# Masking B and the scores by one product, signed sums of dt*A, and another order of the first loads in a modulated Mamba-and-experts layer

## The chip, the cores and the metric

The kernel runs on one core of a Trainium2 chip. The metric is the device time of one execution in microseconds (us); the time before is the median of three runs.

## The reference, cut to what matters

Eight sequences (`B = 8`) of 2048 tokens with 256 features, all in float32. A conditioning vector gives six modulation vectors per sequence. Then, for each sequence:

```python
h = _layernorm(x) * (1 + ca) + sa
x = x + ga * _L0_attn_ref(h, ...)        # the Mamba part
h = _layernorm(x) * (1 + cb) + sb
x = x + gb * _L0_ffn_ref(h, ...)         # 8 experts, weighted by a softmax with a threshold
```

The Mamba part projects `h` to z, xBC and dt, runs a causal convolution of four taps over xBC, applies SiLU, and does a chunked state-space scan with 8 heads of 64 channels and a state of 128:

```python
dt = softplus(dt + dt_bias);  A = -exp(A_log)
dA_cs = jnp.cumsum(dt * A, axis=2)
Lmat = where(causal, exp(dA_cs_i - dA_cs_j), 0)
scores = einsum('bcihn,bcjhn->bcijh', Cc, Bc) * Lmat
states = einsum('bcjhn,bcjh,bcjhp->bchpn', Bc, exp(dA_cs[-1] - dA_cs), xt)
y_off  = einsum('bcihn,bcih,bchpn->bcihp', Cc, exp(dA_cs), prev_states)
```

## The kernel before

The tokens are worked in 32 blocks of 512 (four per sequence), numbered 0 to 31 here; a block has four chunks of 128 tokens. Each stage of a block is a Python generator. `STARTS` gives the planned time of a stage within its block, `PERIOD` (70) the distance of blocks, and `at` and `after` put a generator into a queue of events; a `yield t` hands over to other stages for a planned `t`. Matmul results go to eight PSUM banks, which `take` hands out and `give` returns in planned time. The planned times decide only the order in which instructions are recorded and which bank each uses; the tile framework then reorders them on each engine by its own priorities, and on the chip each engine runs its list in order, held by semaphores. An engine that waits therefore holds everything behind it in its list.

The stages that the change and the prediction touch, with the lines of the profile:

- `condition` (L250) and `modulation` (L257): the conditioning vector is turned (L252), copied (L253, DVE) to `ct`, multiplied with the first modulation weights `wpp` (L262) and copied to `mod_pp` (L267, DVE).
- `first_norm` (L351): statistics of x (L315, L316, DVE), then `modulated` (L318): `rstd` by two POOL instructions (L310, and the power at L311), `shift` (L324, DVE), the normalised `xn` (L328, ACT), transposes (L338, PE), `ht` (L340, ACT). `gate_weights` (L679) calls `modulated` once more in each block, so there are two `shift` steps per block.
- `project_xbc` (L409, PE) and `conv` (L364 and L368 on ACT, three taps at L372 on DVE), `silu_xbc` (L427, ACT), `project_z` (L445, PE; SiLU at L432, ACT).
- `steps_of_time` (L454 on): dt, then `cs` = running sum of dt * `a_pos` (L486, L487), `whole` = minus its last column (L489), `e` = exp(cs + whole) (L493, ACT), three transposes (L497) and `tok_major` by three DVE copies, the second with the sign turned (L502).
- `spread` (L508): a DMA broadcasts `cs` from DRAM to all partitions as `wide` (L512).
- `within` (L517), once per chunk: `w` = Relu(wide + bias) in eight ACT instructions (L527), transposes of x (L537) and of B (L538), scores (L540), two exponentials (L541, L542), then on DVE `xdt` (L545), the masked scores `sm` (L549) and the copy `bm` of the transposed B (L551). `sm` and `bm` read the two halves of the bank `b_ps`, so that bank comes free when both are done. POOL makes `xdec` (L558) and `cw` (L565); DVE `w = w * sm` (L562); PE the new state (L576), POOL and DVE its decay and sum (L579, L590).
- `outputs` (L596): y (L608, PE), plus D times x (L620, DVE), times SiLU(z) (L624, DVE), squares (L631, ACT) and their sums on POOL (L633, L634).
- `output` (L662), `residual` (L671), `gate_weights`, and `experts` (L781 on PE; weighted sums L738 on DVE; L746, L748 on POOL).
- Loads are issued from SP's queue: the modulation weights, block 0's x as one DMA, the input weights, small vectors, and from planned times on the expert weights (`expert_weights`, L170) and the x of later blocks (`fetch`, L105).

Of the kernel before, what the change touches and what calls it, by code (L numbers as in the profile page):

```python
# [11 lines left out]
AF = mybir.ActivationFunctionType  # L12
ALU = mybir.AluOpType
AX = mybir.AxisListType

P = 128
# [9 lines left out]
def kernel(  # L26
# [26 lines left out]
    nc = tc.nc  # L53
    B, L, DM = x.shape
    NPROJ = w_in.shape[1]
    DI = w_out.shape[0]
    NH = dt_bias.shape[0]
# [7 lines left out]
    NC = T // P  # L65
    NSB = L // T
# [6 lines left out]
    def new(pool, shape, tag, bufs=None):  # L73
        n_names[0] += 1
        kw = {} if bufs is None else {"bufs": bufs}
        return pool.tile(shape, F32, tag=tag, name=f"{tag}_{n_names[0]}", **kw)
# [6 lines left out]

    ident = new(const, [P, P], "ident")
    make_identity(nc, ident)
    upper = new(const, [P, P], "upper")
    make_upper_triangular(nc, upper, val=1.0, diag=True)
    ones = new(const, [P, P], "ones")
    nc.gpsimd.memset(ones, 1.0)
    neg_half = new(const, [P, NC], "neg_half")  # L90
    nc.gpsimd.memset(neg_half, -0.5)

# [4 lines left out]
    chk = ctx.enter_context(tc.tile_pool(name="chunk", bufs=2))  # L97
    sml = ctx.enter_context(tc.tile_pool(name="small", bufs=2))
    dram = ctx.enter_context(tc.tile_pool(name="dram", bufs=2, space=bass.MemoryType.DRAM))

    def load(b, s):
        xt = new(io, [P, NC, DM], "xt")
        nc.sync.dma_start(out=xt, in_=x[b, ts(s, T), :].rearrange("(c p) d -> p c d", p=P))  # L105
        return xt

    def columns(dst, src, first, count):
        nc.sync.dma_start(
            out=dst, in_=src[:, first : first + count].rearrange("(k p) n -> p k n", p=P)  # L110
        )
# [22 lines left out]
    heads["gate_b"] = new(const, [P, NE], "gate_b")  # L134
    w_dt = new(const, [P, KD, QD], "w_dt")
    nc.gpsimd.memset(w_dt, 0.0)
    a_pos = new(const, [P, 1], "a_pos")

    columns(wpp[0], wmod, 0, 2 * DM)
    first_x = load(0, 0)  # L140
    columns(w_in_sb[:, :, DI:], w_in, DI, NPROJ - DI)
    with nc.allow_non_contiguous_dma(reason="small vectors, an element or a few per partition"):
        nc.sync.dma_start(out=conv_w_sb, in_=conv_w.rearrange("(m p) k -> p m k", p=P))
        nc.sync.dma_start(out=conv_b_sb, in_=conv_b.rearrange("(m p) -> p m", p=P))
        columns(w_in_sb[:, :, :DI], w_in, 0, DI)
        for name, v in (("dt_bias", dt_bias), ("a_log", a_log)):
            for c in range(NC):
                nc.sync.dma_start(
                    out=heads[name][c * QD : c * QD + NH, :], in_=v.unsqueeze(1)
                )  # L150
        for q in range(2):
            nc.sync.dma_start(
                out=d_ch[ts(q, HEADDIM), :],
                in_=d_skip.rearrange("(m q) -> q m", q=2)[q].partition_broadcast(HEADDIM),
            )
        nc.sync.dma_start(out=norm_sb, in_=norm_w.rearrange("(m p) -> p m", p=P))
        nc.sync.dma_start(out=wo_n, in_=w_out.rearrange("(m p) o -> p m o", p=P))
        for g, part in enumerate((2, 5)):
            columns(wgate[:, :, g, :], wmod, part * DM, DM)
        columns(wpp[1], wmod, 3 * DM, 2 * DM)  # L160
        nc.sync.dma_start(
            out=gate_w_sb[:, :, :NE], in_=gate_w.rearrange("(k p) e -> p k e", p=P)
        )
# [11 lines left out]
    def head_weights():  # L175

        nc.gpsimd.tensor_copy(w_dt[:, :, :NH], w_in_sb[:, :, DI + CD : NPROJ])
        nc.scalar.activation(a_pos, heads["a_log"], AF.Exp)
        yield


# [4 lines left out]
    def at(time, stage):  # L186
        heapq.heappush(events, (time, n_events[0], stage))
        n_events[0] += 1
# [31 lines left out]
    def give(ps):  # L220
        free_at[bank_of.pop(ps.tensor.name)] = clock[0] + READ_TIME

# [2 lines left out]
        while any(step not in d for step in steps):  # L225
            yield 0.2

    order = [(b, s) for b in range(B) for s in range(NSB)]
    info = [{} for _ in order]
    gated, carry = {}, {}  # L230

# [7 lines left out]
        return t.unsqueeze(2).to_broadcast([P, NC, NE])  # L239

    def fetch(n):
        info[n]["x"] = first_x if n == 0 else load(*order[n])
        yield


# [3 lines left out]
    def condition():  # L249
        for k in range(KD):  # L250
            ps = yield from take("m")
            nc.tensor.transpose(ps[:, :B], cond_sb[:, ts(k, P)], ident[:B, :B])  # L252
            nc.vector.tensor_copy(ct[:, k, :], ps[:, :B])  # L253
            give(ps)
        yield from modulation(0)

    def modulation(half):  # L257
        ps = yield from take("m")
        for n in range(2):
            for d in range(KD):  # L260
                for k in range(KD):
                    nc.tensor.matmul(  # L262
                        ps[:, ts(n * KD + d, B)], wpp[half][:, k, n * DM + d * P :][:, :P],
                        ct[:, k, :], start=(k == 0), stop=(k == KD - 1),
                    )
        for n in range(2):
            nc.vector.tensor_scalar(  # L267
                mod_pp[:, 2 * half + n], ps[:, ts(n, KD * B)].rearrange("p (d b) -> p d b", b=B),
                float(n), None, ALU.add,
            )  # L270
        give(ps)
# [180 lines left out]
    def steps_of_time(n):  # L452

        d = info[n]  # L454
        ht = d["ht", 0]
        dt_ps = yield from take("m")
        for k in range(KD):
            for c in range(NC):
                nc.tensor.matmul(
                    dt_ps[ts(c, QD), :P], w_dt[:, k, :], ht[:, k, ts(c, P)],  # L460
                    start=(k == 0), stop=(k == KD - 1), skip_group_check=True,
                )
        yield 1.0


        dtv = new(sml, [P, P], "dtv", bufs=1)
        e = new(sml, [P, P], "sp_e", bufs=1)
        u = new(sml, [P, P], "sp_u", bufs=1)
        ln = new(sml, [P, P], "sp_l", bufs=1)
        dt = new(sml, [P, P], "dt", bufs=1)  # L470
        nc.vector.tensor_scalar(dtv, dt_ps[:, :P], heads["dt_bias"], None, ALU.add)
        give(dt_ps)
        nc.vector.scalar_tensor_tensor(e, dtv, -1.0, dtv, ALU.mult, ALU.min)
        yield 0.6
        nc.scalar.activation(e, e, AF.Exp)
        yield 0.5
        nc.vector.tensor_scalar(u, e, 1.0, None, ALU.add)
        yield 0.3
        nc.scalar.activation(ln, u, AF.Ln)
        yield 1.8  # L480
        nc.vector.scalar_tensor_tensor(u, u, 1.0, e, ALU.subtract, ALU.subtract)
        nc.vector.scalar_tensor_tensor(dt, dtv, 0.0, ln, ALU.max, ALU.add)
        nc.vector.tensor_sub(dt, dt, u)

        cs = new(sml, [P, P], "cs", bufs=1)
        nc.vector.tensor_scalar(u, dt, a_pos, None, ALU.mult)  # L486
        nc.vector.tensor_tensor_scan(cs, ones, u, 0.0, ALU.mult, ALU.add)  # L487
        whole = new(sml, [P, 1], "whole")
        nc.vector.tensor_scalar(whole, cs[:, P - 1 : P], -1.0, None, ALU.mult)  # L489
        yield 4.0  # L490
        d["cs_d"] = new(dram, [P, P], "cs_d")
        nc.sync.dma_start(out=d["cs_d"], in_=cs)
        nc.scalar.activation(e, cs, AF.Exp, bias=whole)  # L493
        yield 7.0
        t_ps = yield from take("m")
        for i, t in enumerate((dt, cs, e)):
            nc.tensor.transpose(t_ps[:, ts(i, P)], t, ident)  # L497
        yield 1.0
        tok_major = d["tok"] = new(sml, [P, 3, NC, NH], "tok_major", bufs=3)
        turned = t_ps[:, : 3 * P].rearrange("p (n c q) -> p n c q", n=3, q=QD)  # L500
        for i, sign in enumerate((1.0, -1.0, 1.0)):
            nc.vector.tensor_scalar(  # L502
                tok_major[:, i], turned[:, i, :, :NH], sign, None, ALU.mult
            )
        give(t_ps)


# [9 lines left out]
    def within(n, c):  # L517
# [7 lines left out]
        w = new(chk, [P, NH, P], "w", bufs=3)  # L525
        for h in range(NH):
            nc.scalar.activation(  # L527
                w[:, h, :], wide[:, h, :], AF.Relu, bias=tok_major[:, 1, c, h : h + 1]
            )
            if h % 4 == 3:  # L530
                yield 1.6
# [6 lines left out]
        nc.tensor.transpose(b_ps[:, :P], bt, ident)  # L538

        nc.tensor.matmul(b_ps[:, P : 2 * P], bt, ct_, start=True, stop=True)  # L540
        nc.scalar.activation(wide, wide, AF.Exp, scale=-1.0)  # L541
        nc.scalar.activation(w, w, AF.Exp, scale=-1.0)  # L542
        yield 1.2
        xdt = new(chk, [P, DI], "xdt", bufs=3)
        nc.vector.tensor_tensor(  # L545
            by_head(xdt), by_head(x_ps[:, :DI]), per_head(tok_major[:, 0, c, :]), ALU.mult
        )
        sm = new(chk, [P, P], "sm")
        nc.vector.tensor_mul(sm, b_ps[:, P : 2 * P], upper)  # L549
        bm = new(chk, [P, P], "bm")  # L550
        nc.vector.tensor_copy(bm, b_ps[:, :P])  # L551
        give(x_ps)
        give(b_ps)
        last = s_of(n) == NSB - 1 and c == NC - 1
# [233 lines left out]


    READ_TIME = 4.5  # L790
    PERIOD, XBC_STEP, Z_STEP, OUT_STEP = 70.0, 6.0, 3.5, 4.4
    STARTS = (
        (fetch, -20.0), (first_norm, -9.0), (project_xbc, 11.5), (project_z, 42.0),
        (silu_xbc, 47.5), (output, 128.0), (gate_weights, 156.0), (experts, 198.0),
    )
    at(-30.0, condition())
    at(12.0, head_weights())
    at(35.0, expert_weights())
    at(20.0, output_weights())
    at(30.0, modulation(1))  # L800
    for n in range(len(order)):
# [42 lines left out]
```

## Time and profile before

| what | value |
|---|---|
| runs shown, median (lowest to highest) | 2406.21 us (2404.78 to 2408.36) |
| the profiled execution's own time | 2408.26 us |
| its span, first to last instruction | 2406.5 us |
| mean granted TensorE clock | 0.988 |
| PE, DVE, ACT, POOL busy | 97%, 76%, 67%, 47% |
| DMA | 110.51 MB, mean 46 GB/s |

A busy share is an average over stages. A line of the timeline gives the start, the duration, the engine, the line of the kernel, the operation with its tiles and shapes, the number of merged instructions, and in brackets the idle time before it with what ended that. "L549" is line 549 of the kernel before; the changed kernel's lines are numbered some ten higher, and this document uses the old numbers for both except in lines copied from the later profile.

### The profile page before, as it was taken

To read this page: it belongs to the slowest core of one execution; us is meant where nothing else is said; L and a number is where in the kernel's file an instruction comes from. 1 tells how busy PE (TensorE), PEld (TensorE's weight loads), DVE (VectorE), ACT (ScalarE), POOL (GpSimd) and SP (SyncE) were. 2 spreads that over 40 slices of the span, in tenths; PEclk is the share of its full clock that TensorE was granted. 3 is DMA by queue.
4 is the path that set the end of the run, shared out by engine and by line. 5 is a ranking of instruction groups with operands and counts; after the bars stand their busy time and mean duration, and the time that the engine had idled before them with its cause. 6 is when DMAs were issued, how large, how long until landed. Compare 5 with 4: busy or idle time off the path is not lost.

```text
span 2406.5 us, 33568 instructions
## 1 busy us (share of the span) xinstructions
PE 2327.3 (97%) x11602; PEld 1313.9 (55%) x11602; DVE 1830.3 (76%) x4414; ACT 1621.4 (67%) x2947; POOL 1128.7 (47%) x1244
## 2 busy tenths in 40 slices
PE   6889999999999999999999999999999999999998
PEld 3545555555555555555555555555555555555564
DVE  4777877777777787777887778777777787778775
ACT  6877676676666766667867667767677667667720
POOL 2554454443554435545445545445545445545442
PEclk8999999999999999999999999999999999999999
DMA  5111011110111101111111111111111111111100
GB/s 164 45 37 39 34 55 45 44 46 28 54 46 44 45 28 54 46 45 54 37 37 54 46 46 53 37 37 55 54 36 54 37 37 54 46 44 45 37 18 18
DMA packets 64601, 110.51 MB, mean 46 GB/s; under 512 B 7048, under 2 KB 47024, under 8 KB 64432
## 3 DMA queue, kind: packets, MB, share of 16 engines
q1 hardware_dynamic: 64416, 108.35, 13.3%
q8 instruction: 93, 1.52, 0.3%
q14 instruction: 76, 0.62, 0.1%
q10 hardware_dynamic: 16, 0.01, 0.0%
HBM read 89.47 MB, written 18.87 MB: 45 GB/s over the span
## 4 chain that ended last, share of the span: by engine, by line
PE 61%; ACT 11%; DVE 7%; POOL 6%; issue 1%; POOLq 0%; ACTq 0%
PE bank L781 26%; PE bank L662 8%; PE bank L409 7%; PE bank L445 6%; PE bank L608 4%; PE bank L576 3%; ACT w L527 3%; DVE xbc L372 2%; POOL cw L565 2%; PE bank L338 1%; PE bank L537 1%; ACT xn L328 1%; POOL rstd L311 1%; ACT wide L541 1%; DVE res L738 1%
## 5 line engine op out<-in xcount | busy, mean ns | idle before, releaser
L781 PE MATMUL bank<-we_sb,ht 128*128 128x512 f32 x2048 | 968.7, 598 | 18.3 <-DVE bm L551 15.6
L738 DVE SCALAR_TENSOR_TENSOR res<-bank,wt,res 128x256 f32<-128x256 f32 x1024 | 487.3, 476 | 212.6 <-PE bank L781 116.5
L781 PEld LDWEIGHTS bank<-we_sb,ht 128*128 128x128 f32 x2048 | 375.5, 191 | 398.8 <-issue 351.8
L372 DVE SCALAR_TENSOR_TENSOR xbc<-bank,conv_w_sb,xbc 128x511 f32<-128x511 f32 (+2 forms) x576 | 425.4, 740 | 96.0 <-ACT halo L368 94.9
L565 POOL TENSOR_TENSOR cw<-wide,xbc 128x1024 f32<-128x1024 f32 x128 | 305.7, 2388 | 274.5 <-ACT wide L541 157.2
L527 ACT ACTIVATE w<-wide,tok_major 128x128 f32<-128x128 f32 x1024 | 327.2, 390 | 137.8 <-PE bank L608 96.2
L409 PE MATMUL bank<-ht,w_in_sb 128*128 128x512 f32 x768 | 375.1, 611 | 5.6 <-DVE xbc L372 4.5
L445 PE MATMUL bank<-ht,w_in_sb 128*128 128x512 f32 x512 | 244.6, 601 | 1.0 <-ACT zs L432 1.0
L662 PE MATMUL bank<-wo,zs 128*128 128x256 f32 x1024 | 244.0, 380 | 0.3
L579 POOL TENSOR_TENSOR state<-state,wide 128x512 f32<-128x512 f32 x112 | 120.8, 1079 | 247.1 <-DVE state L590 216.7
L409 PEld LDWEIGHTS bank<-ht,w_in_sb 128*128 128x128 f32 x768 | 141.9, 194 | 163.6 <-issue 142.1
L340 ACT ACTIVATE ht<-bank,mod_pp 128x512 f32<-128x512 f32 x128 | 97.7, 776 | 188.9 <-PE bank L338 188.8
L364 ACT ACTIVATE xbc<-bank,conv_b_sb,conv_w_sb 128x512 f32<-128x512 f32 x192 | 147.3, 767 | 113.9 <-PE bank L409 113.0
L662 PEld LDWEIGHTS bank<-wo,zs 128*128 128x128 f32 x1024 | 189.9, 191 | 51.2 <-issue 26.4
L746 POOL TENSOR_TENSOR res<-res,gates 128x256 f32<-128x256 f32 x128 | 133.4, 1042 | 149.2 <-DVE res L738 142.4
L558 POOL TENSOR_TENSOR xdec<-xdt,tok_major 128x512 f32<-128x512 f32 x120 | 139.0, 1159 | 132.7 <-DVE xdt L545 130.5
L328 ACT ACTIVATE xn<-xt,shift,rstd 128x256 f32<-128x256 f32 x256 | 137.1, 591 | 89.2 <-DVE shift L324 89.2
L620 DVE SCALAR_TENSOR_TENSOR bank<-xbc,d_ch,bank 128x128 f32<-128x128 f32 x512 | 176.6, 349 | 20.7 <-PE bank L608 11.8
L562 DVE TENSOR_TENSOR w<-w,sm 128x1024 f32<-128x1024 f32 x128 | 189.0, 1477 | 0.0
L633 POOL TENSOR_TENSOR sq<-sq 128x256 f32<-128x256 f32 x128 | 99.2, 775 | 124.4 <-ACT sq L631 124.2
L445 PEld LDWEIGHTS bank<-ht,w_in_sb 128*128 128x128 f32 x512 | 91.0, 191 | 97.6 <-issue 90.6
L576 PE MATMUL bank<-xdec,bm 128*128 128x512 f32 x240 | 130.1, 625 | 12.7 <-POOL xdec L558 6.4
(129 smaller groups left out, 3364.6 us busy)
## 6 DMA issues: line engine op xcount, KB each, us to landing
wide<-cs_d SPq DMA_DIRECT2D x128, 512.0 KB
xt<-_attn_hidden_states_dram SPq DMA_DIRECT2D x32, 512.0 KB
out_dram<-xt SPq DMA_DIRECT2D x32, 512.0 KB
we_sb<-in_L_ffn_expert_w_dram SPq DMA_DIRECT2D x8, 256.0 KB
cs_d<-cs SPq DMA_DIRECT2D x32, 64.0 KB
ht<-in_L_wmod_dram SPq DMA_DIRECT2D x2, 512.0 KB
w_in_sb<-in_L_attn_W_in_dram SPq DMA_DIRECT2D x1, 776.0 KB
w_in_sb<-in_L_attn_W_in_dram SPq DMA_DIRECT2D x1, 512.0 KB
```

The lines of the kernel that those rows point to most:

```text
L328: nc.scalar.activation(xn[:, c, :], src[:, c, :], AF.Identity, bias=shift[:, c : c + 1], scale=rstd[:, c : c + 1],)
L372: nc.vector.scalar_tensor_tensor(acc[:, ahead:], ps[:, : T - ahead], conv_w_sb[:, m, k : k + 1], acc[:, ahead:], ALU.mult, ALU.add,)
L409: nc.tensor.matmul(ps, w_in_sb[:, k, DI + m * P : DI + (m + 1) * P], ht[:, k, :], start=(k == 0), stop=(k == KD - 1),)
L445: nc.tensor.matmul(ps, w_in_sb[:, k, ts(m, P)], ht[:, k, :], start=(k == 0), stop=(k == KD - 1),)
L527: nc.scalar.activation(w[:, h, :], wide[:, h, :], AF.Relu, bias=tok_major[:, 1, c, h : h + 1])
L562: nc.vector.tensor_tensor(w, w, sm[:, None, :].to_broadcast([P, NH, P]), ALU.mult)
L565: nc.gpsimd.tensor_tensor(cw, wide, ct_[:, None, :].to_broadcast([P, NH, P]), ALU.mult)
L576: nc.tensor.matmul(st_ps[:, :DI], bm, xdec, start=True, stop=True)
L620: nc.vector.scalar_tensor_tensor(y[:, m, :], xbc[:, m, tok], d_ch[:, m : m + 1], y[:, m, :], ALU.mult, ALU.add,)
L662: nc.tensor.matmul(o_ps[:, :DM], d["zs"][:, m, ts(c, P)], wo[:, m, :], start=(m == 0), stop=(m == MI - 1),)
L738: nc.vector.scalar_tensor_tensor(res, ps[:, ts(q, DM)], wt[:, c, e + q : e + q + 1], res, ALU.mult, ALU.add)
L781: nc.tensor.matmul(ps, ht[:, k, ts(c, P)], we_sb[:, k, e : e + per, :].rearrange("p e o -> p (e o)"), start=(k == 0), stop=(k == KD - 1),)
```

## The change

The `upper` mask and the `ones` become two halves of one tile, so that one DVE product over 256 columns makes B (times ones) and the masked scores (times upper) where there were a product and a copy of 128 columns each. dt * A is summed with its negative sign, so that the turned sums need no change of sign: three copies to `tok_major` become one, `whole` goes, and the signs move into scales of ACT instructions; one small POOL instruction negates exp(A_log) once. At the start, block 0's x is loaded first, as four DMAs, block 1's x is loaded among the weights, and the expert weights' planned time goes from 35 to 60. `ct` is copied by ACT instead of DVE. The first modulation's copies are recorded later, and 15 products of the two masks that nobody reads (`warm`) are put on PE.

```diff
-    upper = new(const, [P, P], "upper")
+    masks = new(const, [P, 2, P], "masks")
+    ones, upper = masks[:, 0, :], masks[:, 1, :]
...
+    first_x = new(io, [P, NC, DM], "xt")
+    for c in range(NC):
+        nc.sync.dma_start(out=first_x[:, c, :], in_=x[0, ts(c, P), :])
     columns(wpp[0], wmod, 0, 2 * DM)
-    first_x = load(0, 0)
     columns(w_in_sb[:, :, DI:], w_in, DI, NPROJ - DI)
...
+        second_x = load(*order[1])
         nc.sync.dma_start(out=norm_sb, in_=norm_w.rearrange("(m p) -> p m", p=P))
...
-        nc.scalar.activation(a_pos, heads["a_log"], AF.Exp)
+        nc.scalar.activation(a_neg, heads["a_log"], AF.Exp)
+        nc.gpsimd.tensor_scalar(a_neg, a_neg, -1.0, None, ALU.mult)
...
-            nc.vector.tensor_copy(ct[:, k, :], ps[:, :B])
+            nc.scalar.copy(ct[:, k, :], ps[:, :B])
...
+        yield from modulation(0, 30.0)
+
+    def warm():
+        ps = yield from take("m")
+        yield 40.9
+        for _ in range(WARM):
+            nc.tensor.matmul(ps[:, :P], ones, upper, start=True, stop=True)
+        give(ps)
...
-        nc.vector.tensor_scalar(u, dt, a_pos, None, ALU.mult)
+        nc.vector.tensor_scalar(u, dt, a_neg, None, ALU.mult)
         nc.vector.tensor_tensor_scan(cs, ones, u, 0.0, ALU.mult, ALU.add)
-        whole = new(sml, [P, 1], "whole")
-        nc.vector.tensor_scalar(whole, cs[:, P - 1 : P], -1.0, None, ALU.mult)
...
-        nc.scalar.activation(e, cs, AF.Exp, bias=whole)
+        nc.scalar.activation(e, cs, AF.Exp, bias=cs[:, P - 1 : P], scale=-1.0)
...
-        for i, sign in enumerate((1.0, -1.0, 1.0)):
-            nc.vector.tensor_scalar(
-                tok_major[:, i], turned[:, i, :, :NH], sign, None, ALU.mult
-            )
+        nc.vector.tensor_copy(tok_major, turned[:, :, :, :NH])
...
-                w[:, h, :], wide[:, h, :], AF.Relu, bias=tok_major[:, 1, c, h : h + 1]
+                w[:, h, :], wide[:, h, :], AF.Relu, bias=tok_major[:, 1, c, h : h + 1], scale=-1.0
...
-        nc.scalar.activation(wide, wide, AF.Exp, scale=-1.0)
+        nc.scalar.activation(wide, wide, AF.Exp)
...
-        sm = new(chk, [P, P], "sm")
-        nc.vector.tensor_mul(sm, b_ps[:, P : 2 * P], upper)
-        bm = new(chk, [P, P], "bm")
-        nc.vector.tensor_copy(bm, b_ps[:, :P])
+        both = new(chk, [P, 2, P], "both")
+        nc.vector.tensor_mul(both, b_ps[:, : 2 * P].rearrange("p (n i) -> p n i", n=2), masks)
+        bm, sm = both[:, 0, :], both[:, 1, :]
...
+    WARM = 15
...
-    at(35.0, expert_weights())
+    at(-30.0, warm())
+    at(60.0, expert_weights())
```

More of the change, by code (lines that the diff above doesn't have):

```diff
@@ L85 @@
     make_identity(nc, ident)
-    upper = new(const, [P, P], "upper")
+    masks = new(const, [P, 2, P], "masks")
+    ones, upper = masks[:, 0, :], masks[:, 1, :]
+    nc.gpsimd.memset(ones, 1.0)
     make_upper_triangular(nc, upper, val=1.0, diag=True)
-    ones = new(const, [P, P], "ones")
-    nc.gpsimd.memset(ones, 1.0)
     neg_half = new(const, [P, NC], "neg_half")
@@ L99 @@
     dram = ctx.enter_context(tc.tile_pool(name="dram", bufs=2, space=bass.MemoryType.DRAM))
+    order = [(b, s) for b in range(B) for s in range(NSB)]
     def load(b, s):
@@ L136 @@
     nc.gpsimd.memset(w_dt, 0.0)
-    a_pos = new(const, [P, 1], "a_pos")
+    a_neg = new(const, [P, 1], "a_neg")
+    first_x = new(io, [P, NC, DM], "xt")
+    for c in range(NC):
+        nc.sync.dma_start(out=first_x[:, c, :], in_=x[0, ts(c, P), :])
     columns(wpp[0], wmod, 0, 2 * DM)
-    first_x = load(0, 0)
     columns(w_in_sb[:, :, DI:], w_in, DI, NPROJ - DI)
@@ L226, in until @@
             yield 0.2
-    order = [(b, s) for b in range(B) for s in range(NSB)]
     info = [{} for _ in order]
@@ L241, in fetch @@
     def fetch(n):
-        info[n]["x"] = first_x if n == 0 else load(*order[n])
+        info[n]["x"] = (first_x, second_x)[n] if n < 2 else load(*order[n])
         yield
@@ L252, in condition, with modulation @@
             nc.tensor.transpose(ps[:, :B], cond_sb[:, ts(k, P)], ident[:B, :B])
-            nc.vector.tensor_copy(ct[:, k, :], ps[:, :B])
+            nc.scalar.copy(ct[:, k, :], ps[:, :B])
             give(ps)
-        yield from modulation(0)
-    def modulation(half):
+        yield from modulation(0, 30.0)
[5 more added lines that the diff above has]
+        give(ps)
+    def modulation(half, later=1.0):
         ps = yield from take("m")
@@ L265, in modulation @@
                     )
+        yield later
         for n in range(2):
```

## The prediction

> **What bounds the kernel now.** I read the page's shares first, then the waits of PE, then a table of windows by groups of four blocks, then the timeline where PE waits.
>
> ```profile
> PE 2327.3 (97%) x11602; PEld 1313.9 (55%) x11602; DVE 1830.3 (76%) x4414; ACT 1621.4 (67%) x2947; POOL 1128.7 (47%) x1244
> PE bank L781 <- DVE bm L551: 15.6, 8, 3.1
> PE bank L649 <- POOL sqs L634: 8.4, 5, 3.4
> PE bank L409 <- DVE xbc L372: 4.5, 5, 3.8
> 680.30:980.50 300.20, 290.66 (x1447) 164.65 (x1446) 232.01 (x551) 203.10 (x369) 140.37 (x154) 0.98 0.13 44
> 980.50:1273.40 292.90, 288.04 (x1447) 162.99 (x1446) 231.39 (x557) 202.48 (x370) 140.69 (x154) 0.99 0.13 45
> 1273.40:1562.20 288.80, 286.72 (x1448) 162.30 (x1447) 225.67 (x552) 202.11 (x369) 141.44 (x154) 1.00 0.13 44
> ```
>
> The window rows begin with start:end and length, then busy time of PE, its weight loads, DVE, ACT and POOL; each holds four blocks (cut at the first L649 of every fourth block). Undisturbed, four blocks take 288.80 us with PE busy 286.72: PE is the bound, and work taken off DVE is worth nothing there. So only PE's waits can be won: 11.4 us more in 680 to 980, 4.1 in 980 to 1273, 5.9 in the 294.70 us of 385.60 to 680.30, and those of the first 385 us. Most of the first three are four copies of one event:
>
> ```profile
> 710.43 0.72 POOL L633 TENSOR_TENSOR sq<-sq 128x256 f32<-128x256 f32 x1 [6.20 <-ACT sq L631]
> 711.92 1.02 POOL L311 TENSOR_TENSOR rstd<-rstd,neg_half 128x4 f32<-128x4 f32 x1
> 712.91 2.34 POOL L565 TENSOR_TENSOR cw<-wide,xbc 128x1024 f32<-128x1024 f32 x1
> 712.97 2.30 DVE L324 SCALAR_TENSOR_TENSOR shift<-mv,rstd 128x4 f32<-128x4 f32 x1 [3.87 <-POOL rstd L311]
> 717.25 0.28 DVE L551 COPY bm<-bank 128x128 f32<-128x128 f32 x1
> 717.58 3.56 PE L781 MATMUL bank<-we_sb,ht 128*128 128x512 f32 x4 [3.15 <-DVE bm L551]
> 720.98 0.60 PE L338 MATMUL bank<-ident,xn 128*128 128x128 f32 x4
> ```
>
> POOL's list holds the power L311 behind the squares' sum, which waits for ACT. DVE's list has `shift` at its head, so DVE stands 3.87 us; then `shift` starts just after `cw` and takes 2.30 us where its shortest is 0.14. Behind it stand L372, L545, L549, L551; PE's next L781 needs the bank that L551 frees: 3.15 us idle, then four matmuls in 3.56 instead of 1.88. The same returns at 793.86 (3.14), 868.57 (3.15) and 1017.80 (3.14).
>
> **Part 1, order on POOL and DVE.** The built changed kernel was compared with before engine by engine. From block 3 on PE's order is the same. But at these four places POOL has both rstd pairs ahead of L633, and DVE has `shift` some ten instructions later, behind L549's successor. By the rows: mv is there at 708.8, so rstd and power end at 710.1 (0.20 + 1.02), ahead of the squares; `cw` meets no `shift`; the merged product ends at about 712.9 and PE, due at 714.43, doesn't wait. The later `shift` (about 721) is needed by ACT only at 727.07. Gain: idle 3.15 + 3.14 + 3.15 + 3.14 = 12.6, and half-speed matmuls after them 1.7 + 0.1 + 2.4 + 1.8 = 6.0 (at 793.86 four took 1.98): 18.6 as an upper end. The windows say 11.4 + 4.1 = 15.5, since undisturbed blocks keep small waits; 0.81 at 1091.94 is no part of it, so I take 14.8. Lower end, one of the four left: 11.
>
> The Trainium skill (SBUF — State Buffer, "two separate sides") says that a DVE instruction with two SBUF inputs and a GpSimd instruction that reads SBUF lock each other out for the whole instruction. It agrees with 2.30 beside 2.34, and speaks against counting on shorter DVE work where the two meet: by it the event that part 2 finds keeps its full length.
>
> **Part 2, the same event made elsewhere.** In block 7 the change does the opposite. Before, `shift` comes late there (571.27, 3.31 of idle) and L409 waits at 575.48 for 3.77 with four matmuls in 3.75: the 5.9 us above. Changed, POOL's list is L633, L310, L634, L311, `cw`, and `shift` stands ahead of L624, two taps, L545 and the product. By the rows: squares from about 561.1, power to 563.65, `shift` to 566.0, the product to 569.7 instead of 564.85. The next user of its bank is L497, at 566.05 before: 3.65 idle plus some 1.7 at half speed, 5.4. The old wait at 575 loses its cause. Net 0; from -4 (as short as the 0.96 at 420.22) to +5 (both).
>
> At two more places `shift` moves ahead of the product (660.08 and 960.29 before). The power ends at 654.59, and bm was ready at 656.00 for an L781 at 656.19: some 0.3 each, less the shorter product. +0.4.
>
> **Part 3, the cheaper instructions.**
>
> ```profile
> L549 DVE TENSOR_TENSOR sm<-bank,upper 128x128 f32<-128x128 f32 x128 | 35.8, 280 | 1.0 <-PE bank L540 1.0
> L551 DVE COPY bm<-bank 128x128 f32<-128x128 f32 x128 | 35.8, 279 | 0.0
> L545 DVE TENSOR_TENSOR xdt<-bank,tok_major 128x512 f32<-128x512 f32 x128 | 87.6, 684 | 26.0 <-PE bank L537 25.9
> ```
>
> Between 128 columns (0.280) and 512 (0.684) a column costs 1.05 ns, so 256 cost 0.415: 0.144 less than the pair, 18.4 us in 128 chunks. Three copies of 0.176 become one of 96 columns, about 0.25 (between 0.176 at 32 and 0.280 at 128): 8.9 us; `whole` 32 x 0.14 = 4.5. Together 31.8 us of DVE's 1830, beside a full PE: nothing, except where PE waits for bm anyway (420.22, 493.38, 1091.94, 52.05): 4 x 0.144 = 0.6. If DVE were the bound, all 31.8 would count. Scales on ACT cost nothing; POOL's negation costs like L177's 0.19 while POOL is idle until 18.38.
>
> **Part 4, the start.**
>
> ```profile
> 15.44 3.78 PE L409 MATMUL bank<-ht,w_in_sb 128*128 128x512 f32 x4 [0.66 <-ACT ht L340]
> 43.34 0.43 DVE L315 BATCH_NORM_STATS2 stats<-xt 128x6 f32<-128x256 f32 x1 [2.53 <-DMA xt<-_attn_hidden_states_dram]
> 48.15 2.29 DVE L324 SCALAR_TENSOR_TENSOR shift<-mv,rstd 128x4 f32<-128x4 f32 x1 [0.87 <-POOL rstd L311]
> 52.05 2.05 PE L576 MATMUL bank<-xdec,bm 128*128 128x512 f32 x2 [4.90 <-DVE bm L551]
> ```
>
> L262 started at 7.98 because the `ct` copies stood behind the statistics on DVE. ACT copies them now at about 4.5, so L262 waits for wpp, issued behind four x loads (each some 0.5 of SP's time) but inside the same first megabyte, which landed by 6.04: about 6.4, some 1.6 earlier. That moves `shift` and xn 1.5 earlier. PE then meets `warm`: 4 of the 15 products before and among the transposes, 11 (22 passes of 0.107 warm or 0.213 at half speed, by L338's and L409's rates) between the transposes' end near 13 and the first L409: 2.4 to 4.7, so L409 starts between 15.4 and 17.7. Before it started at 15.44 and four passes took 3.70 to 19.14 instead of 1.71, as good as a warm start at 17.43. Worth -2.0 to +2.3 (if still at half speed); I take -0.6.
>
> The Trainium skill (TensorE: Matmul & The Clock Gate, "What's actually happening") counts a busy window of about 3.4 us, whatever is issued in it. By it 16 passes are slow and 6 fast, L409 starts at 17.1, and the term is -0.3; and unread products use up a window in which the real ones would have advanced at half speed.
>
> Block 1's x is there early, so the 2.53 goes; ACT loads one table fewer (1.28) before block 1's xn, since e's exponential stands before the first SiLU. What is late next is the statistics of block 2, ahead of block 1's `shift` in DVE's list, whose x now comes behind seven expert loads (3.4 MB from about 31 on; at the 267 GB/s at which 2.88 MB landed by 43.3, near 44.5; needed near 44.3). `shift` still meets `cw`. I take 1.6 of the 2.53, from 0 to 2.5.
>
> Blocks 0 to 2 have other order changes on all engines, beside some 20 us of PE idle between 62 and 385. I see no sign, so 0, from -4 to +4.
>
> **Sum.** -14.8 + 0 + 0.4 - 0.6 - 0.6 - 1.6 = -17.2. The profiled execution took 2408.3, which gives 2391.1; it lies 2.05 above the median of the runs, so I predict 2389.
>
> **Rivals.** (A) A wait takes the place of those removed: block 7 keeps both, one of the four stays or moves, the ramp loses some: -17.2 + 5 + 4 = 2397 to 2401. For it: part 2 shows that order alone makes such events. Against it: from block 15 on the orders repeat as before, whose windows are clean. 0.15. (B) No change, 2404: if PE at these four places is held by something that the profile doesn't name behind bm. Against it: L551 ends 0.05 us before L781 starts. 0.06. (C) Slower, 2414: in blocks 0 to 2 DVE's list now has the softmax steps L714 to L720 between the y additions L620; a wait for ACT's exponential (L712) then holds the y banks and PE's L608. Each such event costs 3.15 + 1.7 = 4.85; it takes five of them to outweigh the gain and reach 2414, deciding from the fourth. Only 7.5 us in all were waited for there before. 0.05. (D) More gain, 2380: block 7's event is short and the ramp wins 4. 0.12. The forecast, 2384 to 2395: 0.62.
>
> Range 2381 to 2399: about 1 in 10 above (B, C and part of A), 1 in 10 below (part of D). A measurement of this kernel can tell about 0.2%, 4.8 us, from no change. Faster by more: forecast, D and nearly all of A, 0.88; same 0.07; slower 0.05.
>
> **What would show it.** Right: four-block windows near 289 us from 680 on; no L781 wait of 3 us for the merged product after block 7; one of 3 to 4 us on L497 in block 7; `shift` near 0.16 in blocks 9 to 13; DVE about 32 us less busy; first L409 at 15.4 to 17.7 with later ones at full rate. Wrong: the four events still there, new PE waits of 3 us in 680 to 1300, PE's idle in 60 to 385 grown by over 10, or a product far above 0.415.

## The result, and the profile after

The changed kernel takes 2383.02 us (median of its runs, 2380.73 to 2383.07) against 2406.21: ratio 0.9902, 95% interval 0.9891 to 0.9912, so 23.2 us less. The forecast was 2389 with a range of 2381 to 2399. Its profiled execution took 2381.93 with a span of 2380.1 and a mean granted clock of 0.993 (before 0.988), 26.4 of span less than the profiled one of before, which lay 2 us above its median.

The first L649 of a block serves as a mark again. Cut there, with the marks read to a tenth, the 26.4 us come from these stretches ("block 2" below is the stretch from block 1's mark to block 2's):

| stretch | before | after | difference |
|---|---|---|---|
| to block 0's mark | 98.0 | 93.6 | -4.4 |
| block 0's mark to block 1's | 62.2 | 63.4 | +1.2 |
| block 1's to block 2's | 78.5 | 72.4 | -6.1 |
| block 2's to block 4's | 146.9 | 146.5 | -0.4 |
| blocks 4 to 8 | 294.7 | 293.8 | -0.9 |
| blocks 8 to 16 | 593.1 | 573.8 | -19.3 |
| blocks 16 to 28 | 866.4 | 869.7 | +3.3 |
| rest | 266.7 | 266.9 | +0.2 |

The windows by groups of four blocks, the first from block 4's mark (start:end, length, busy time of PE, its weight loads, DVE, ACT, POOL):

```profile
375.90:669.70 293.80, 287.66 (x1447) 163.35 (x1446) 225.20 (x519) 201.27 (x367) 141.85 (x154) 0.99 0.14 46
669.70:954.90 285.20, 285.20 (x1448) 162.65 (x1447) 225.11 (x523) 203.00 (x369) 140.85 (x154) 1.00 0.14 46
954.90:1243.50 288.60, 286.33 (x1447) 162.32 (x1446) 229.03 (x528) 201.83 (x369) 139.47 (x154) 1.00 0.14 45
1243.50:1533.50 290.00, 286.79 (x1448) 162.30 (x1447) 225.69 (x524) 202.03 (x369) 140.70 (x154) 1.00 0.14 45
```

The second row is new to both kernels: PE is busy for 285.20 of 285.20 us. The 288.80 that the prediction took for undisturbed was not the floor; it still held 2.1 us of waits, and 1.5 more of PE's own time. The fourth row is worse than before's 288.80.

PE's waits (us in total, times, longest):

```profile
PE bank L586 <- POOL xdec L568: 12.8, 22, 1.5
PE bank L659 <- POOL sqs L644: 6.0, 4, 3.4
...
PE bank L511 <- DVE both L560: 3.1, 1, 3.1
```

The eight waits of 15.6 for `bm` have become 1.9 in three. The waits of L576 (now L586) for `xdec` were 6.4 in 13. The first of the four places, in the timeline:

```profile
698.42 1.01 POOL L326 TENSOR_TENSOR rstd<-rstd,neg_half 128x4 f32<-128x4 f32 x1
700.14 0.74 POOL L643 TENSOR_TENSOR sq<-sq 128x256 f32<-128x256 f32 x1 [0.72 <-ACT halo L383]
...
701.37 2.39 POOL L575 TENSOR_TENSOR cw<-wide,xbc 128x1024 f32<-128x1024 f32 x1
701.41 0.41 DVE L560 TENSOR_TENSOR both<-bank,masks 128x256 f32<-128x256 f32 x1
...
708.76 0.14 DVE L339 SCALAR_TENSOR_TENSOR shift<-mv,rstd 128x4 f32<-128x4 f32 x1
```

The power ends before the squares' sum begins, the product runs beside `cw` without being held, and `shift` follows 7 us later in 0.14. Block 7 has the event instead:

```profile
553.46 1.02 POOL L326 TENSOR_TENSOR rstd<-rstd,neg_half 128x4 f32<-128x4 f32 x1
554.45 2.35 POOL L575 TENSOR_TENSOR cw<-wide,xbc 128x1024 f32<-128x1024 f32 x1
554.51 2.30 DVE L339 SCALAR_TENSOR_TENSOR shift<-mv,rstd 128x4 f32<-128x4 f32 x1 [3.66 <-POOL rstd L326]
...
559.64 0.41 DVE L560 TENSOR_TENSOR both<-bank,masks 128x256 f32<-128x256 f32 x1
...
560.10 0.33 PE L511 MATMUL bank<-ident,dt 128*128 128x128 f32 x1 [3.07 <-DVE both L560]
```

And from block 13 on, once in four blocks, something that the prediction did not have:

```profile
1351.43 1.56 POOL L644 TENSOR_TENSOR sqs<-sq 128x128 f32<-128x128 f32 x1
...
1352.95 1.04 POOL L568 TENSOR_TENSOR xdec<-xdt,tok_major 128x512 f32<-128x512 f32 x1
...
1354.05 1.13 PE L586 MATMUL bank<-xdec,both 128*128 128x512 f32 x2 [1.47 <-POOL xdec L568]
```

`xdec` stands behind the second sum of the squares, whose first half waited 0.74 for ACT (L643 at 1350.63); in before's list it stood ahead of L634, and PE did not wait there.

### The profile page after: what moved, and what is told of

The parts are those of the page before. It is cut to its first block, busy times and chain, and to the rows that moved or that the text cites. A ratio compares the mean times of both kernels' runs of the same rounds, so it can differ in the third digit from the quotient of the medians.

```text
span 2380.1 us, 33341 instructions
## 1 busy us (share of the span) xinstructions
PE 2317.9 (97%) x11632; PEld 1313.3 (55%) x11632; DVE 1816.6 (76%) x4188; ACT 1621.7 (68%) x2950; POOL 1128.4 (47%) x1245
## 4 chain that ended last, share of the span: by engine, by line
PE 61%; ACT 10%; POOL 9%; DVE 6%; issue 1%; POOLq 0%; ACTq 0%; DVEq 0%
PE bank L791 26%; PE bank L672 8%; PE bank L424 7%; PE bank L460 6%; PE bank L618 4%; POOL cw L575 3%; PE bank L586 3%; ACT w L538 3%; DVE xbc L387 2%; PE bank L353 1%; PE bank L548 1%; ACT xbc L442 1%; POOL xdec L568 1%; POOL sq L643 1%; ACT wide L552 1%
## 5 line engine op out<-in xcount | busy, mean ns | idle before, releaser
L575 POOL TENSOR_TENSOR cw<-wide,xbc 128x1024 f32<-128x1024 f32 x128 | 310.8, 2428 | 295.3 <-ACT wide L552 168.8
L424 PE MATMUL bank<-ht,w_in_sb 128*128 128x512 f32 x768 | 369.1, 603 | 0.8 <-DVE xbc L387 0.8
L460 PE MATMUL bank<-ht,w_in_sb 128*128 128x512 f32 x512 | 244.4, 601 | 0.0
L572 DVE TENSOR_TENSOR w<-w,both 128x1024 f32<-128x1024 f32 x128 | 191.6, 1497 | 1.4
L586 PE MATMUL bank<-xdec,both 128*128 128x512 f32 x240 | 128.6, 618 | 17.6 <-POOL xdec L568 12.8
L643 POOL TENSOR_TENSOR sq<-sq 128x256 f32<-128x256 f32 x128 | 98.0, 766 | 91.3 <-ACT sq L641 73.4
```

The source lines that it names most:

```text
L424: nc.tensor.matmul(ps, w_in_sb[:, k, DI + m * P : DI + (m + 1) * P], ht[:, k, :], start=(k == 0), stop=(k == KD - 1),)
L460: nc.tensor.matmul(ps, w_in_sb[:, k, ts(m, P)], ht[:, k, :], start=(k == 0), stop=(k == KD - 1),)
L572: nc.vector.tensor_tensor(w, w, sm[:, None, :].to_broadcast([P, NH, P]), ALU.mult)
L575: nc.gpsimd.tensor_tensor(cw, wide, ct_[:, None, :].to_broadcast([P, NH, P]), ALU.mult)
L586: nc.tensor.matmul(st_ps[:, :DI], bm, xdec, start=True, stop=True)
```

## The experiments

Two theories ran against each other. ORDER: the gain is where instructions stand in POOL's and DVE's lists. WORK: the gain is the DVE time that the cheaper instructions save. Times are medians; each is compared with runs of the kernel before on the same chip, which had medians of 2406.07 to 2406.80.

**One part at a time.** First the product alone:

```diff
+        both = new(chk, [P, 2, P], "both")
+        nc.vector.tensor_mul(both, b_ps[:, : 2 * P].rearrange("p (n i) -> p n i", n=2), masks)
...
-        nc.vector.tensor_copy(bm, b_ps[:, :P])
```

> The kernel before with the merged product alone (masks side by side, one DVE product of 256 columns; signs, tok_major and the start as before). Two theories. ORDER: the change gains because DVE's and POOL's instructions stand in another order at four places in blocks 9 to 13 (18 us by the four-block windows of before and after) and in the ramp; cheaper DVE instructions are worth next to nothing. WORK: the gain is DVE's shorter instructions, wherever they are, so each part gains by its share of the 31.8 us that the prediction counted (product 18.4, signs and copies 13.4). In this kernel POOL's list still has the squares' sum straight ahead of the power at the same four places, and shift ahead of the product, as before. ORDER expects the four waits of PE on L781 still there, about 3.0 us each, and 2399 to 2406 us (only the ramp, whose list is like that of the changed kernel from block 2 on, can gain, at most 6). WORK expects a gain of 18.4 / 31.8 of 23.2, 13 us: 2393.

Measured: 2412.51, ratio 1.0035 (1.0022 to 1.0047): slower by 6.2. The four waits are there, 3.08 each. One of them, and a wait of block 2 that is longer than before's (1.67), in the timeline:

```profile
169.61 0.48 PE L648 MATMUL bank<-ident,sqs 128*128 128x128 f32 x1 [3.20 <-POOL sqs L633]
...
721.11 1.13 PE L780 MATMUL bank<-we_sb,ht 128*128 128x512 f32 x2 [3.08 <-DVE both L549]
```

The part that gives the change its name saves 18.7 us of DVE records and makes the kernel slower, because blocks 1 and 2 get longer (66.0 and 80.5 between marks, before 62.2 and 78.5). DVE's busy time does not fall with the records: it is 1830.4 (1830.3 before), since the products `w = w * sm` take 196.7 in all instead of 189.0. WORK, which counted records and wanted 2393, missed by 19.5; ORDER's range missed by 6, since it let the ramp only gain.

Then the signs alone:

```diff
-        nc.vector.tensor_scalar(u, dt, a_pos, None, ALU.mult)
+        nc.vector.tensor_scalar(u, dt, a_neg, None, ALU.mult)
...
-        nc.vector.tensor_scalar(whole, cs[:, P - 1 : P], -1.0, None, ALU.mult)
...
+        nc.vector.tensor_copy(tok_major, turned[:, :, :, :NH])
```

> The kernel before with the signs alone (negated A, no whole, one copy to tok_major, scales of -1 on ACT; product and copy of B apart, start as before). Here POOL's list at the four places is that of the changed kernel, and shift stands behind the product. ORDER expects no L781 wait over 1 us in blocks 9 to 13, four-block windows of 285 to 290 us from block 8 on, and a gain of 15 to 21 us: 2385 to 2391. WORK expects 13.4 / 31.8 of 23.2, 10 us: 2396.

Measured: 2387.25, ratio 0.9922 (0.9909 to 0.9936): 19.0 less, as ORDER said. No wait over 1 us is left between blocks 8 and 13, and the window is the full one, with product and copy apart as before:

```profile
676.30:961.50 285.20, 285.20 (x1448) 162.70 (x1447) 224.06 (x539) 203.13 (x370) 140.96 (x154) 1.00 0.14 46
```

The later windows are 289.8, so the `xdec` waits come with the signs too.

The start alone (the front's diff of loads, `ct`, modulation and `warm`):

> The kernel before with the start alone (order of the loads, block 1's x early, expert weights planned at 60, ct copied by ACT, the first modulation's copies later, the unread products); DVE's product and signs as before. DVE's and POOL's lists from block 2 on are those of the kernel before. ORDER expects the four waits still there and only the gain of the first two blocks, 3.3 to 4.4 us at the first L649 of blocks 0 and 1: 2401 to 2404. WORK gives it nothing, as no DVE work goes: 2406. A third reading, that the whole difference of 9.7 us at block 2 comes from the start, expects 2396 to 2397.

Measured: 2400.84, ratio 0.9981 (0.9973 to 0.9990): 5.4 less, with an interval of 2.4 to 6.5. The four waits are at 711.51, 787.90, 862.60 and 1011.86, 3.14 each. From block 0's mark on the profile is that of before, 78.5 in block 2 included, so the third reading is out. ORDER's 2401 to 2404 is met to within 0.2.

The loads without the rest of the start:

```diff
+    for c in range(NC):
+        nc.sync.dma_start(out=first_x[:, c, :], in_=x[0, ts(c, P), :])
...
+        second_x = load(*order[1])
...
-    at(35.0, expert_weights())
+    at(60.0, expert_weights())
```

> The kernel before with the loads' order alone (block 0's x first and in four pieces, block 1's x early, expert weights planned at 60), without ct on ACT, the later modulation copies and the unread products. The whole start gave 5.4 us (2400.84 against 2406.28). If the loads carry it (block 1's statistics no longer wait for x, 2.53 us in the profile of before), 2401 to 2403.5 and no DVE wait for xt near 43. If the earlier modulation and the warm products carry it, 2404.5 to 2406.5.

Measured: 2403.58, ratio 0.9989 (0.9980 to 0.9998): 3.2 less, at the edge between the two expectations. A wait of 2.4 for x is still in DVE's list. The parts of the start can't be told apart at this resolution.

The changed kernel with its start undone:

> The changed kernel with its start undone (the kernel before with product and signs). The start alone was worth 5.4 us (2400.84 against 2406.28), signs alone 19.0, and the product alone cost 6.2. If the parts simply add, this kernel is 2406.3 - 19.0 + 6.2 = 2393.5, and the whole change would be 2388, where it is 2383. If the product's cost (new waits in blocks 1 and 2 for the squares and xdec) is an effect of order that does not appear together with the signs, it is 2383.0 + 5.4 = 2388.4, within 1.5.

Measured: 2385.74, ratio 0.9913 (0.9899 to 0.9926). The parts don't add: the sum of the single ones would have been 2393.5. The other reading, 2388.4 within 1.5, is nearer and misses by 1.2. The product, which cost 6.2 alone, costs nothing beside the signs (2385.74 against 2387.25). The reason is in block 2: 80.5 with the product, 76.8 with the signs, 72.4 with both, as in the changed kernel. Of the two L649 waits of 1.62 and 1.67 that before has there, the signs alone leave one; with both parts both are gone. The next run shows that this is not the parts' doing alone.

**DVE's work given back.**

```diff
         bm, sm = both[:, 0, :], both[:, 1, :]
+        pad = new(chk, [P, P], "pad")
+        nc.vector.tensor_copy(pad, b_ps[:, :P])
```

> The changed kernel with one useless DVE copy of 128 columns out of the same bank behind each merged product (128 copies of some 0.28 us, 36 us of DVE in all, more than the 18.4 that the merged product saves), so that DVE has more to do than before and the bank comes free later. Lists of DVE and POOL are otherwise those of the changed kernel at the four places. ORDER expects 2383 to 2387 (a few waits on the bank longer by 0.2 to 0.3). WORK expects the product's gain gone and more: 2396 to 2409.

Measured: 2384.22, ratio 0.9915 (0.9902 to 0.9929): 1.2 above the changed kernel, less than the two intervals can tell apart. The four places stay free (285.2 for blocks 8 to 12), so 128 copies more cost next to nothing there. Two things limit what this run shows. DVE's busy time rose by only 3.9, to 1820.5, still under before's 1830.3, since the `w` products took 177.7 in all instead of 191.6; it does not show what a DVE as busy as before would cost. And the sum hides a loss: block 2 takes 78.7 instead of 72.4, nearly made up by shorter stretches elsewhere. The two L649 waits of before are back, although product and signs are both in:

```profile
157.21 0.33 PE L661 MATMUL bank<-ident,sqs 128*128 128x128 f32 x1 [1.62 <-POOL sqs L646]
159.20 0.33 PE L661 MATMUL bank<-ident,sqs 128*128 128x128 f32 x1 [1.67 <-POOL sqs L646]
```

**Order alone.** One planned pause, and not one instruction more or less:

```diff
         inv_sqrt(rstd, mv[:, :, 1], 1.0)
-        yield 3.0
+        yield 4.0
```

> The kernel before with one planned time changed: in modulated the pause between the power and shift is 4.0 instead of 3.0. Not one instruction is added, removed or shortened; only the lists' order changes: at the four places in blocks 9 to 13, and in block 7, POOL no longer has the squares' sum straight ahead of the power. ORDER expects the four L781 waits of 3.1 gone and block 7's too: 2383 to 2392, if the new order makes no waits of its own in the later blocks (which repeat with another pattern than before, so up to 8 us more are possible). WORK, for which the gain needs fewer or shorter DVE instructions, expects 2406.

Measured: 2440.00, ratio 1.0145 (1.0131 to 1.0159): slower by 34. The four waits of blocks 9 to 13 are gone as expected (blocks 8 to 12 take 288.1 instead of 300.2). Block 7's wait on L409 is not (3.75 at 569.12), and from block 13 on each four blocks bring three new ones of 2.8 to 3.8, and four blocks take 301 to 304. One of them:

```profile
1066.95 1.01 POOL L311 TENSOR_TENSOR rstd<-rstd,neg_half 128x4 f32<-128x4 f32 x1
...
1067.99 0.68 DVE L324 SCALAR_TENSOR_TENSOR shift<-mv,rstd 128x4 f32<-128x4 f32 x1 [4.28 <-POOL rstd L311]
...
1071.36 1.22 PE L781 MATMUL bank<-we_sb,ht 128*128 128x512 f32 x1 [3.28 <-DVE xdt L545]
```

Here the `rstd` pair stands behind `cw` in POOL's list, `shift` holds DVE for 4.28, and xdt is late for PE. The expectation allowed 8 us for new waits and had no ground for that bound. WORK's 2406 misses too: order alone moves this kernel by more than the whole change did.

**DVE not held by POOL.** Before, with `shift` on POOL behind the power:

```diff
-        nc.vector.scalar_tensor_tensor(shift, mv[:, :, 0], -1.0, rstd, ALU.mult, ALU.mult)
+        nc.gpsimd.tensor_tensor(shift, mv[:, :, 0], rstd, ALU.mult)
+        nc.gpsimd.tensor_scalar(shift, shift, -1.0, None, ALU.mult)
```

> The kernel before with shift computed on POOL by two small instructions behind the power (product of mean and rstd, then times -1) instead of one on DVE. POOL's list still has the squares' sum ahead of the power at the four places, but DVE has no instruction that waits for it. If DVE standing behind POOL is the chain that PE pays for, the four L781 waits go (18 us) although the squares are as late as before: 2386 to 2392, with at most 5 us given back where two more POOL instructions (0.4 us, 64 times) delay cw or xdec. If instead POOL's own lateness (cw, xdec) is what PE waits for, nothing goes: 2404 to 2410. It also shows what becomes of the 2.30 us that shift takes beside cw.

Measured: 2395.95, ratio 0.9960 (0.9948 to 0.9973). The four waits are gone, although the squares' sum still stands ahead of the power:

```profile
704.18 0.72 POOL L634 TENSOR_TENSOR sq<-sq 128x256 f32<-128x256 f32 x1 [6.76 <-ACT sq L632]
...
705.80 1.04 POOL L311 TENSOR_TENSOR rstd<-rstd,neg_half 128x4 f32<-128x4 f32 x1
...
706.69 0.28 DVE L552 COPY bm<-bank 128x128 f32<-128x128 f32 x1
...
707.40 2.38 POOL L566 TENSOR_TENSOR cw<-wide,xbc 128x1024 f32<-128x1024 f32 x1
```

The copy that frees the bank ends before `cw` begins; DVE no longer stands behind the power. Blocks 8 to 16 take 578.6 instead of 593.1, and block 7's wait on L409 is gone. So the chain that the prediction named is the cause, not POOL's lateness. More is given back than expected: `xdec` waits of 2.83 and 3.49 in blocks 1 and 2, one of 2.16 in block 7, and one of 1.71 in every second block from 14 on.

**The held instruction by itself.** `shift` as four instructions of one column, with rstd as the per-partition scalar:

```diff
+        for c in range(NC):
+            nc.vector.tensor_scalar(
+                shift[:, c : c + 1], mv[:, c, 0:1], rstd[:, c : c + 1], -1.0, ALU.mult, ALU.mult
+            )
```

> The kernel before with shift made by four DVE instructions of one column each (mean from one SBUF tensor, times rstd as the per-partition scalar, times -1) instead of one with two SBUF tensors. Only the duration of these instructions is read; the lists' order is another one than before, so the time says nothing. If any read of SBUF by DVE is held while POOL runs cw, the one that starts beside cw takes up to 2.3 us as shift did. If only an instruction with two SBUF tensors is held, each of the four takes 0.07 to 0.15 us beside cw too.

Measured, in the timeline:

```profile
48.05 0.58 DVE L325 TENSOR_SCALAR shift<-mv,rstd 128x1 f32<-128x1 f32 x4 [0.87 <-POOL rstd L311]
...
47.98 2.35 POOL L568 TENSOR_TENSOR cw<-wide,xbc 128x1024 f32<-128x1024 f32 x1
```

At the same point, beside the same `cw`, the one instruction of before took 2.29 (48.15); the four take 0.58 together, and no one of the 256 takes more than 0.215 (each 0.18 to 0.215, a little above the 0.07 to 0.15 that was expected). In the kernel before, five of the 64 `shift` start while `cw` runs, and all five take 2.29 to 2.30; here five of the 256 do, and they take 0.20 to 0.21. So the form with two SBUF tensors is what is held, not any read by DVE.

This run also parts the two halves of the event, DVE standing for the power and `shift` being held. Its lists have a place (another one than before's four) where `shift` stands behind a late power without being held:

```profile
417.49 0.21 DVE L325 TENSOR_SCALAR shift<-mv,rstd 128x1 f32<-128x1 f32 x1 [4.12 <-POOL rstd L311]
...
420.78 3.78 PE L784 MATMUL bank<-we_sb,ht 128*128 128x512 f32 x4 [3.64 <-DVE bm L554]
```

DVE stands 4.12 and PE still waits 3.64: the place in the list is enough. At before's four places both halves add up; there the hold, 2.30 instead of 0.14, would by these rows (an estimate) be some 2.2 of the 3.15.

The time of this single run, 2388.41, belongs to another order of the lists and does not price `shift`. It does speak against WORK: DVE is busy for 1844.0, 13.7 more than before, and the kernel is 18 faster.

**The unread products.**

```diff
-    WARM = 15
+    WARM = 0
```

> The changed kernel without the 15 unread products (WARM 0), all else equal. The prediction took them and the earlier L262 together for -0.6 us. Without them the first L424 starts about 2.8 us earlier (near 13.9) and its first four passes run at half speed (about 3.7 instead of 1.88), with later ones perhaps slow too. If the products only fill a wait and move the warm-up, 2382 to 2385 and the first L586 within 1 us of 48.46. If the warm clock that they give carries into the first blocks, 2386 to 2390.

Measured: 2381.47, ratio 0.9902 (0.9887 to 0.9917), 1.6 under the time with them, within what the intervals leave open, and 0.5 under the lower reading. The first four L409 passes, without and with:

```profile
14.12 3.78 PE L424 MATMUL bank<-ht,w_in_sb 128*128 128x512 f32 x4 [0.66 <-ACT ht L355]
```

```profile
16.70 1.88 PE L424 MATMUL bank<-ht,w_in_sb 128*128 128x512 f32 x4
```

They run at full speed after the products, but start 2.6 later; the step after them is at 17.83 without and at 18.51 with. The products warm PE at the price of the time that the real passes would have used for it. The first L586 comes at 46.46 without them, after a wait of 1.01, and at 48.46 with them, after 3.41; the expectation had it within 1 us. At block 1's mark 0.9 of these 2.0 us are left.

**A better order.** The changed kernel with the pause ahead of `xdec` changed, first to 0.4:

```diff
-        yield 1.0
+        yield 0.4
         if not last:
             xdec = new(chk, [P, DI], "xdec", bufs=1)
```

> The changed kernel with one planned time changed: the pause ahead of xdec is 0.4 instead of 1.0. POOL's list then has xdec ahead of the squares' sum more often, and at block 7 the power no longer stands behind it. ORDER expects block 7's L511 wait of 3.07 and its half-speed matmuls gone (3 to 5 us) and the L586 waits for xdec of 1.1 to 1.5 in every fourth block gone (1 us each four blocks, 3 to 4 us): 2375 to 2380. The rival, that these two are not on the path (PE would only wait elsewhere), expects 2382 to 2384.

Measured: 2392.52, ratio 0.9947 (0.9935 to 0.9960): slower than the changed kernel by 9.5. Block 7's wait is gone (72.4 instead of 77.4 between marks, with 76.3 instead of 73.2 in the stretch ahead of it), but `xdec` is now waited for 27.2 us in 26 times, and block 2 takes 80.0 instead of 72.4. Both readings missed.

Then to 1.1:

```diff
-        yield 1.0
+        yield 1.1
         if not last:
             xdec = new(chk, [P, DI], "xdec", bufs=1)
```

> The changed kernel with the pause ahead of xdec 1.1 instead of 1.0. In POOL's list xdec no longer stands behind the squares' second sum at the four places from block 13 on where L586 waits 1.1 to 1.5 us; block 7 is as in the changed kernel. ORDER expects those waits gone, four-block windows from block 16 on of 288.8 to 289.2 instead of 289.9, and 2379 to 2381. The miss of the 0.4 pause (nine new or longer waits for xdec and the squares in blocks 1 to 13) says that another order may make as many waits as it takes away: that reading expects 2383 to 2393.

Measured: 2368.83, ratio 0.9849 (0.9835 to 0.9862): 14.2 better than the changed kernel and 38 better than before. Every window between blocks 8 and 28 is now PE without a gap:

```profile
956.80:1242.10 285.30, 285.30 (x1447) 162.57 (x1446) 224.69 (x523) 202.98 (x369) 140.85 (x154) 1.00 0.14 46
1242.10:1527.30 285.20, 285.20 (x1448) 162.64 (x1447) 224.70 (x523) 203.04 (x369) 140.86 (x154) 1.00 0.14 46
```

The expectation of 2379 to 2381 missed because it took 288.8 to 289.2 for the floor, as the prediction had; a window without a gap, like that of the changed kernel's blocks 8 to 12, now repeats to block 28.

## Why the prediction was right, and where not

**The four events (-14.8): right in mechanism, too small.** Measured -19.3 in blocks 8 to 16. The upper end of the step, 18.6 from idle time and half-speed matmuls, was the better price. The mis-sized term is the floor, 288.8: it was read from the windows that followed, and those had waits of their own; 285.2 was reached. (15.5 less 0.81 is also 14.7, not 14.8.) The signs alone brought the new order and the gain; with `shift` on POOL the four waits went while the squares stayed where they were, so DVE standing behind the power, and then held beside `cw`, was the cause, and rival B is out. That saved work brings the gain is refuted by runs in which the time does not follow DVE's busy time: `shift` in four parts (13.7 us busier than before, 18 faster), the pause of 1.1 (1816.5 busy against the changed kernel's 1816.6, 14.2 faster) and the pause of 4.0 (not one instruction changed, 34 slower).

**Block 7 (0): right.** A wait of 3.07 on L497 where 3.65 was forecast, then four L409 passes in 3.39; the wait at 575 gone; net -0.9 over blocks 4 to 8.

**The cheaper instructions: 31.8 of DVE, worth 0.6.** The worth was right in that no run shows a gain from them that an order of the lists does not explain; the 0.6 itself is too small to be measured. The amount was not right: DVE's busy time fell by 13.7. The records themselves came as forecast:

```profile
L560 DVE TENSOR_TENSOR both<-bank,masks 128x256 f32<-128x256 f32 x128 | 52.9, 414 | 1.5 <-PE bank L551 1.5
L339 DVE SCALAR_TENSOR_TENSOR shift<-mv,rstd 128x4 f32<-128x4 f32 x64 | 14.3, 224 | 44.7 <-POOL rstd L326 44.6
```

But a record overlaps the next by some 0.08 us. From start to start, L549 and L551 took 0.20 each and the product takes 0.33: 0.07 saved a chunk, not 0.144; the three copies 0.33 and now 0.17. By these rates product and copies are worth 9.0 + 5.1, not 18.4 + 8.9. Even that is not what the 13.7 consists of: `shift` gave 6.5 (20.8 in all before, 14.3 now, with two of 64 held instead of five), and the `w` products took 2.6 back (189.0, now 191.6). The Trainium skill has the overlap (Perfetto Trace Analysis, "Optimizing Scalar/DVE Operations"): the fixed part of a DVE instruction shows in its profiled latency at about twice what it keeps the engine, since the half that acknowledges the write overlaps with the next instruction. The trace agrees in kind: the overlap is 0.08 of 0.28 and 0.08 of 0.41, the same at both widths.

**The start (-0.6 and -1.6): the place right, the size open.** The first L409 came at 16.70 where 15.4 to 17.7 was forecast, at full rate. The wait of 2.53 for x near 43 is gone, and `shift` meets `cw` at 44.48 (48.15 before) for 2.31, as forecast. The product passes ahead of it took 2.78 for 22, by the rates used 18 fast and 4 slow; the count worked out from the Trainium skill's window, 6 fast, was too low. To block 1's mark the profiles differ by 3.2, but kernels with the start of before had block 0's mark anywhere between 91.8 and 98.4, so one profile can't size it. The start alone gave 2.4 to 6.5 and, taken out of the changed kernel, 2.7 (with overlapping intervals): the forecast 2.2 lies just under that. No run shows the unread products to be worth anything: without them the time is 2381.47.

**Blocks 0 to 2, "I see no sign, so 0": wrong by 6.1, outside the term's own end of 4.** The sign was in the first fence: L649 waits 8.4 us for POOL's sums in five times, and two of these, 1.62 and 1.67 at 162 and 164, were priced nowhere. In the changed kernel both are gone, and in the padded one, with one more DVE copy in each chunk, both are back. So this gain is not owed to product and signs as such; whether the lists' order or a few tenths of DVE's time decides it, and by which instruction, was not isolated.

**"From block 15 on the orders repeat as before": wrong by +3.3.** POOL's list there has `xdec` behind the second sum once in four blocks. This is rival A's mechanism at a part of its price.

**The sum.** Between the profiled executions the forecast was 2391.1 and 2381.9 came, 9.2 less: -4.5 for the four events, -6.1 in block 2, -1.0 at the start, -0.9 around block 7, +3.3 in the later blocks. By medians it is 6.0, since the profiled execution of before was 2.05 above its median and that of after 1.1 below. The result lies 1 us under the forecast's own band of 2384 to 2395, towards rival D: its gain in the ramp came, its short event in block 7 did not.

Rival C did not come: no L608 wait in blocks 0 to 2 is longer than before's 2.35 at block 0.

## What to carry to other kernels

On engines that run their lists in order, look for an instruction that waits for another engine and stands ahead of one that frees what the bound engine needs; where it stands was worth -19 us here, the work saved beside a full PE too little to be told from the noise. Any edit, even an instruction less, lets the scheduler write other lists: compare them at every place, later blocks too, and treat one planned pause as a parameter to be measured (one moved the kernel before by +34 us, another the changed kernel by +9 and by -14). The floor of a stage is the window in which the bound engine has no gap (285.2), not the best window that the kernel happens to have (288.8).

## What the runs showed of the hardware

- A DVE instruction with two SBUF tensors took 2.29 us beside POOL's `cw`, and 0.13 to 0.17 elsewhere in the kernel before; four with one tensor and a per-partition scalar took 0.58 beside it. The Trainium skill (SBUF — State Buffer, "two separate sides") names the two SBUF inputs as the condition, and another page of it (DVE: scalar operands, raw-bit mode, write accounting and state across instructions, "Scalar operands") says that such a scalar does not take up the second tensor stream. The run agrees with both. The prediction had weighed the lock and not this way out of it.
- After an idle of 3.07 us PE ran the next four 512-column passes in 3.39 instead of 1.88; after one of 1.47 its next two took 1.13, against 1.02. The length of the idle alone doesn't decide: after 3.14 at 793.86 in the kernel before four passes took 1.98, and after 3.15 at 868.57 they took 3.78.
- The merged product, with `masks` in SBUF and the bank in PSUM as inputs, took its 0.41 us beside `cw` (701.41): one SBUF tensor, not held.
